# A Perceiver block: pools of their own for gates and ups, the last two pairs of chunks by sequence, and an early table of roots

## The chip, the cores and the metric

The kernel runs on one core of a Trainium2 chip. The metric is device time in microseconds (us) of one execution, a median over runs. Beside the runs there is one profiled execution, whose trace gives start, length and waits of every instruction. The engines are TensorE (PE in the trace, PEld for its weight loads), VectorE (DVE), ScalarE (ACT), GpSimd (POOL) and SyncE (SP, which issues most of the transfers).

## The reference

Four sequences of 128 tokens with 1024 features pass through cross-attention over 8192 context rows, causal self-attention, and a feed-forward part, each behind a layernorm and added to its input. The change touches only the last part:

```python
gate_up = jnp.einsum('bsh,oh->bso', x, w_gu)
gate, up = (gate_up[..., :I], gate_up[..., I:])        # I = 2816
h = jax.nn.silu(gate) * up
y = jnp.einsum('bsi,hi->bsh', h, w_down)
rms = jnp.sqrt(jnp.mean(y * y, axis=-1, keepdims=True) + EPS)
return y / rms
```

The weights `w_gu` and `w_down` come packed in 4 bits with a scale for each group of 128. The block's output is x plus this.

## The kernel before

The kernel is one function, `tile_perceiver`. Its earlier stages (keys and values of the context, cross-attention, projections, self-attention) are issued in an order written out by hand: steps with a due time go to an agenda, which `perform()` issues sorted. The weights of the feed-forward part are unpacked meanwhile and kept in DRAM as f32 (`gu_d`, `dn_d`). The last step of the agenda is `first_gate_up` (L1253), the 48 matmuls of gate and up of the first chunk of inner features, into PSUM tiles of the pool `acc_ps`. After that the order within each engine is not written by hand: the framework orders the instructions from their dependencies, their place in the program and its own estimate of times, and it puts in all waits.

The 2816 inner features are 22 chunks of 128 (NI = 22). All 512 tokens (four sequences t of 128) are the moving operand of the gates and ups, so a gate or an up of one chunk is a tile of 128 features by 512 tokens.

Products are made of three matmuls, to get more precision than one gives: each f32 operand is split in a high part (ScalarE, L155), a low part (VectorE, L158) and a third part (VectorE, L159). The high and low products go to accumulator a, the third to accumulator b, and `join_into` puts them together: ScalarE scales a into `fa` (L1386), VectorE adds b (L1387).

The feed-forward part:

- `load_ffn` (L1378 and after) brings 128x1024 weights from DRAM (`fw_raw`, issued by SP) and splits them in `fw_h`, `fw_l` and `fw_d`. All these have two buffers.
- Chunk 0 is joined from `acc_ps` by `inner(0, ...)`. Then the pools `sa_ps` (transposes and values of self-attention: three tiles `pt` and one `po`, on the default side of PSUM) and `acc_ps` (two `a` and two `b`, on the right side) are closed, and `gu_ps` is opened, which takes all eight banks: gate_a, gate_b, up_a, up_b, two of each.
- For j = 1 to 21: load gate weights, 24 matmuls; load up weights, 24 matmuls (`matmul_halves`, L165); then `inner(j, ...)`: join gate, join up, sigmoid (L1411), two products (L1412, L1413) into `hT[j]`. For j under 8 (EARLY) `hT[j]` is split at once by `split_inner` (ScalarE L1399, VectorE L1400 to L1403).
- Then `gu_ps` is closed, the memory of `x3` and of the gates is given back, and the pools `ff_h` (SBUF) and `y_ps` (PSUM, eight banks: y_a and y_b for each of four sequences) are opened.
- The downs: for each half n of the 1024 output columns, for each of 11 pairs q of chunks: load the pair's weights, and for each sequence t six matmuls (L1454, two chunks by three parts). In the first half the remaining `hT` (8 to 21) are split along the way.
- After each half, for each t: join into `y` (L1387), Square with a sum over the columns (L1465). In the second half also: sum of both halves (L1468), mean (L1469), root on ScalarE (L1472), reciprocal (L1473), and for both halves the final step `y * ms + x1` (L1476) and the transfer to the output (L1479).

ScalarE's root needs another table of functions than the sigmoid; a table load stands in the trace as ACT_TABLE_LOAD.

Of the kernel before, what the change touches and what calls it, by code (L numbers as in the profile page):

```python
# [34 lines left out]
F32 = mybir.dt.float32  # L35
# [5 lines left out]
AF = mybir.ActivationFunctionType  # L41
ALU = mybir.AluOpType
AX = mybir.AxisListType
PSUM = bass.MemoryType.PSUM
DRAM = bass.MemoryType.DRAM

P = 128
# [24 lines left out]
NI = INNER // P  # L72
# [14 lines left out]
def tile_perceiver(  # L87
# [26 lines left out]
    nc = tc.nc  # L114
# [15 lines left out]
    dn_d = dram.tile([2, NI // 2, P, 2, 512], F32, name="dn_d")  # L130
# [13 lines left out]
    def split(src, hi, lo, df):  # L144

        split_hi(src, hi)
        split_lo(src, hi, lo, df)
# [8 lines left out]
    def matmul_halves(a, b, lhs, rhs):  # L161

        for k in range(NC):
            for i, ps in enumerate((a, a, b)):
                nc.tensor.matmul(  # L165
                    ps,
                    lhsT=lhs(i, k),
                    rhs=rhs(i, k),
                    start=(k == 0 and i != 1),
                    stop=(k == NC - 1 and i != 0),  # L170
                )
# [41 lines left out]
    w3 = {0: [], 1: []}  # L213
# [489 lines left out]
    first, last = V_QUANT  # L703
# [30 lines left out]
    with tc.tile_pool(name="at_e", bufs=1) as at_e, tc.tile_pool(  # L734
        name="at_s", bufs=4
    ) as small, tc.tile_pool(name="at", bufs=2) as at, tc.tile_pool(
        name="at_ps", bufs=3, space=PSUM
# [219 lines left out]
        with tc.manual_schedule():  # L957
            for s in range(n_steps + LAG_V):
                n, g = divmod(s, NSC)
# [9 lines left out]
                if n < len(units):  # L969
                    h, t = units[n]  # L970
# [43 lines left out]
    w3s = {}  # L1014
# [356 lines left out]
    with tc.tile_pool(name="ff_t", bufs=2) as ff_t, tc.tile_pool(name="ff", bufs=1) as ff:  # L1371
        hT = [ff.tile([P, 512], F32, name=f"hT{j}", tag=f"hT{j}") for j in range(NI)]
        ss = ff.tile([P, NT, 2], F32, name="ss")

        def load_ffn(src, n):

            raw = ff_t.tile([P, C], F32, name="fw_raw", tag="fw_raw")
            nc.sync.dma_start(out=raw.rearrange("p (i n) -> p i n", n=n), in_=src)  # L1378
            parts = [ff_t.tile([P, C], F32R, name=f"fw_{c}", tag=f"fw_{c}") for c in "hld"]
            split(raw, *parts)  # L1380
            return [t.rearrange("p (i n) -> p i n", n=n) for t in parts]

        def join_into(dst, a, b):

            fa = ff_t.tile([P, 512], F32, name="fa", tag="fa")
            nc.scalar.mul(fa, a, 1.0 + 1.0 / UP)  # L1386
            nc.vector.scalar_tensor_tensor(dst, b, -1.0 / UP, fa, ALU.mult, ALU.add)  # L1387

        def joined(pool, a, b, name):
            t = pool.tile([P, 512], F32, name=name, tag=name)  # L1390
            join_into(t, a, b)
            return t


        h3 = {}

        def split_inner(pool, j):
            hi, lo = (pool.tile([P, 512], F32R, name=f"h3_{c}{j}") for c in "hl")
            nc.scalar.mul(hi, hT[j], 1.0 - 0.5 / UP)  # L1399
            nc.vector.tensor_tensor(lo, hT[j], hi, ALU.subtract)  # L1400
            nc.vector.tensor_scalar_mul(lo, lo, UP)
            df = ff.tile([P, 512], F32R, name=f"h3_d{j}", tag=f"hT{j}")
            nc.vector.tensor_tensor(df, hi, lo, ALU.subtract)  # L1403
            h3[j] = [hi, lo, df]

        with tc.tile_pool(name="ff_g", bufs=2) as ff_g:

            def inner(j, gate_ab, up_ab):
                gate, up = joined(ff_g, *gate_ab, "gate"), joined(ff_g, *up_ab, "up")
                sg = ff_g.tile([P, 512], F32, name="sg", tag="sg")  # L1410
                nc.scalar.activation(sg, gate, AF.Sigmoid)  # L1411
                nc.vector.tensor_tensor(sg, sg, gate, ALU.mult)  # L1412
                nc.vector.tensor_tensor(hT[j], sg, up, ALU.mult)  # L1413
                if j < EARLY:
                    split_inner(ff, j)

            inner(0, acc["ff", 0], acc["ff", 1])
            sa_ps_s.close()
            acc_s.close()
            with tc.tile_pool(name="gu_ps", bufs=2, space=PSUM) as gu_ps:  # L1420
                for j in range(1, NI):
                    gu = []
                    for i, name in enumerate(("gate", "up")):
                        w3 = load_ffn(gu_d[2 * j + i], P)
                        ab = [
                            gu_ps.tile([P, 512], F32, name=f"{name}_{c}", tag=f"{name}_{c}")
                            for c in "ab"
                        ]
                        matmul_halves(
                            *ab, lambda i, k: w3[i][:, k, :], lambda i, k: x3[i][:, :, k, :]  # L1430
                        )
                        gu.append(ab)
                    inner(j, *gu)
        x3_s.close()

        with tc.tile_pool(name="ff_h", bufs=1) as ff_h, tc.tile_pool(
            name="y_ps", bufs=1, space=PSUM
        ) as y_ps:
            y = ff_h.tile([P, NT, C], F32, name="y")
            for n in range(2):  # L1440
                yab = [
                    [y_ps.tile([P, 512], F32, name=f"y{t}_{c}", tag=f"y{t}_{c}") for c in "ab"]
                    for t in range(NT)
                ]
                for q in range(NI // 2):
                    w3 = load_ffn(dn_d[n, q], 512)
                    if n == 0:
                        for j in range(2 * q + 2, min(2 * q + 4, NI)):
                            if j >= EARLY:
                                split_inner(ff_h, j)  # L1450
                    for t in range(NT):
                        for j in (2 * q, 2 * q + 1):
                            for i, ps in enumerate((yab[t][0], yab[t][0], yab[t][1])):
                                nc.tensor.matmul(  # L1454
                                    ps,
                                    lhsT=h3[j][i][:, ts(t, P)],
                                    rhs=w3[i][:, j % 2, :],
                                    start=(j == 0 and i != 1),
                                    stop=(j == NI - 1 and i != 0),
                                )  # L1460
                for t in range(NT):
                    yt = y[:, t, ts(n, 512)]
                    join_into(yt, *yab[t])
                    sqr = ff_h.tile([P, 512], F32, name="sqr", tag="sqr")
                    nc.scalar.activation(sqr, yt, AF.Square, accum_out=ss[:, t, n : n + 1])  # L1465
                    if n == 1:
                        ms = ff.tile([P, 1], F32, name="ms", tag="ms", bufs=NT)
                        nc.vector.tensor_tensor(ms, ss[:, t, 0:1], ss[:, t, 1:2], ALU.add)  # L1468
                        nc.vector.tensor_scalar(  # L1469
                            ms, ms, 1.0 / C, 1e-6 / FP4_UP**2, ALU.mult, ALU.add  # L1470
                        )
                        nc.scalar.activation(ms, ms, AF.Sqrt)  # L1472
                        nc.vector.reciprocal(ms, ms)  # L1473
                        for m in range(2):
                            yt = y[:, t, ts(m, 512)]
                            nc.vector.scalar_tensor_tensor(  # L1476
                                yt, yt, ms, x1[:, t, ts(m, 512)], ALU.mult, ALU.add
                            )
                            nc.sync.dma_start(out=out[ts(t, P), ts(m, 512)], in_=yt)  # L1479
# [71 lines left out]
```

## Time and profile before

| what | us |
|---|---|
| median of 3 runs (2878.3 to 2881.0) | 2880.05 |
| profiled execution, its own time | 2883.89 |
| its span, first to last instruction | 2882.1 |
| TensorE busy in the span | 2666.1 (93%) |
| VectorE busy | 2418.6 (84%) |
| ScalarE busy | 1266.1 (44%) |
| first gate matmul of chunk 1 starts | 2508.8 |
| last up matmul starts | 2743.9 |
| last down matmul starts | 2870.5 |

Times in the trace count from the first instruction. In a row of the trace's groups stand line, engine, operation, output and inputs, shape and count, then busy time and mean length of one, and after the second bar how long the engine had been idle just before those instructions and what ended that. Matmuls overlap their neighbours, so a length of 394 ns is longer than the distance of two starts; distances of starts are the better measure of TensorE's pace.

### The profile page before, as it was taken

How to read it: one execution, taken by the hardware profiler on the slowest of the kernel's cores; microseconds unless marked ns; L12 is line 12 of the kernel's file. 1: busy time of each engine (PE TensorE's matmuls, PEld its weight loads, DVE VectorE, ACT ScalarE, POOL GpSimd, SP SyncE). 2: the span in 40 equal slices, each digit the busy share in tenths (PEclk: the TensorE clock that was granted, in tenths of full speed). 3: DMA queues.
4: the chain of work that ended last, by engine and by line, in shares of the span. 5: the costliest groups of instructions: out<-in, count | busy, mean ns of one | idle time of the engine just before them, and what ended most of it. 6: DMA issues, size and time to landing. Idle time of an engine off the chain costs nothing.

```text
span 2882.1 us, 41034 instructions
## 1 busy us (share of the span) xinstructions
PE 2666.1 (93%) x15480; PEld 2067.8 (72%) x15480; DVE 2418.6 (84%) x3959; ACT 1266.1 (44%) x1399; POOL 454.6 (16%) x608
## 2 busy tenths in 40 slices
PE   8999999999999999999987877787778899799998
PEld 3788888888888888888864555555555777688876
DVE  6899999555799989898879999999986898676674
ACT  4211212121323333333219999999983245333332
POOL 0011111000012222222122233322311000000000
PEclk9999999999999999999998999999999999899999
DMA  5555565222348777777437788878882322122222
GB/s 186 168 198 199 199 211 211 95 95 95 135 125 205 193 191 186 192 181 198 108 87 162 143 167 163 170 161 154 159 167 87 95 70 67 52 95 92 92 91 91
DMA packets 452711, 413.17 MB, mean 143 GB/s; under 512 B 356953, under 2 KB 361625, under 8 KB 452513
## 3 DMA queue, kind: packets, MB, share of 16 engines
q1 hardware_dynamic: 404928, 252.22, 36.6%
q0 software_dynamic: 46528, 157.29, 17.2%
q8 instruction: 121, 1.98, 0.3%
q10 hardware_dynamic: 1056, 1.05, 0.2%
q14 instruction: 78, 0.63, 0.1%
HBM read 220.14 MB, written 104.34 MB: 113 GB/s over the span
## 4 chain that ended last, share of the span: by engine, by line
PE 71%; DVE 20%; issue 4%; POOL 2%; ACT 1%; DMA 1%; SPq 0%; DVEq 0%; ACTq 0%; POOLq 0%
PE kv_a L342 33%; PE kv_b L342 16%; DVE e L787 13%; PE acc_a L1100 3%; PE y_a L1454 3%; PE gate_a L165 3%; PE up_a L165 3%; POOL sk L760 2%; PE acc_b L1100 2%; PE y_b L1454 1%; PE gate_b L165 1%; PE up_b L165 1%; PE q_ps L292 1%; PE a_pt L830 1%; PE sc L780 1%
## 5 line engine op out<-in xcount | busy, mean ns | idle before, releaser
L342 PE MATMUL kv_a<-w_h,c_h 128*128 128x512 f32 x2048 | 806.3, 394 | 0.0
L342 PE MATMUL kv_a<-w_l,c_l 128*128 128x512 f32 x2048 | 806.0, 394 | 0.2 <-ACT w_l L246 0.2
L342 PE MATMUL kv_b<-w_d,c_d 128*128 128x512 f32 x2048 | 806.0, 394 | 0.0
L787 DVE CUSTOM_DVE_ANT_0 e<-sc,sk 128x1024 f32<-128x1024 f32 x512 | 593.2, 1219 | 8.8 <-PE sc L780 7.7
L815 ACT ACTIVATE a<-e,m,sqs 128x4096 int16<-128x4096 f32 x128 | 486.9, 3804 | 25.2 <-DVE m L804 24.8
L342 PEld LDWEIGHTS kv_a<-w_l,c_l 128*128 128x128 f32 x2048 | 384.8, 188 | 89.6 <-ACT w_l L246 0.6
L342 PEld LDWEIGHTS kv_a<-w_h,c_h 128*128 128x128 f32 x2048 | 384.9, 188 | 88.9 <-issue 0.2
L342 PEld LDWEIGHTS kv_b<-w_d,c_d 128*128 128x128 f32 x2048 | 384.8, 188 | 88.9 <-DVE c_d L159 0.3
L155 ACT ACTIVATE c_h<-c_raw 128x1024 fp32r<-128x1024 f32 x128 | 135.1, 1057 | 415.8 <-PE kv_a L342 413.5
L356 DVE SCALAR_TENSOR_TENSOR f<-kv_a,bkv 128x512 f32<-128x512 f32 x256 | 175.6, 686 | 163.3 <-PE kv_a L342 162.6
L780 PE MATMUL sc<-kt,qT 64*128 64x512 bf16 x1024 | 207.4, 397 | 102.5 <-DVE mx L787 98.5
L581 ACT CAST kst<-kT 128x512 bf16<-128x512 int16 x128 | 89.4, 698 | 309.0 <-DMA kT<-ki 309.0
L830 PE MATMUL a_pt<-ident,a 128*128 128x128 f32 x1024 | 176.5, 297 | 20.7 <-ACT a L815 16.1
L357 DVE SCALAR_TENSOR_TENSOR f<-kv_b,f 128x512 f32<-128x512 f32 x256 | 176.6, 690 | 20.3 <-DVE f L356 0.9
L760 POOL PARTITION_BROADCAST sk<-sk_row x120 | 142.5, 1297 | 312.9 <-DVE mx L787 312.7
L830 PEld LDWEIGHTS a_pt<-ident,a 128*128 128x128 f32 x1024 | 113.0, 146 | 87.2 <-ACT a L815 48.6
L780 PEld LDWEIGHTS <-qT 64*128 64x128 bf16 x1024 | 74.8, 93 | 130.9 <-issue 101.2
L158 DVE TENSOR_TENSOR fw_l<-fw_raw,fw_h 128x1024 fp32r<-128x1024 f32 x64 | 78.2, 1223 | 107.1 <-ACT fw_h L155 106.9
L158 DVE TENSOR_TENSOR c_l<-c_raw,c_h 128x1024 fp32r<-128x1024 f32 x128 | 155.6, 1215 | 6.2 <-ACT c_h L155 5.9
L159 DVE SCALAR_TENSOR_TENSOR c_d<-c_l,c_raw 128x1024 fp32r<-128x1024 f32 x128 | 156.2, 1220 | 2.3
L155 ACT ACTIVATE fw_h<-fw_raw 128x1024 fp32r<-128x1024 f32 x64 | 67.8, 1061 | 179.7 <-PE y_a L1454 75.1
L548 ACT CAST vq<-vi 128x1024 f16<-128x1024 int16 x64 | 66.9, 1046 | 174.2 <-DVE vi L541 128.8
(203 smaller groups left out, 4114.1 us busy)
## 6 DMA issues: line engine op xcount, KB each, us to landing
c_raw<-in_ctxT SPq DMA_DIRECT2D x128, 512.0 KB, 3.6
v_d<-f POOLq DMA_DIRECT2D x64, 512.0 KB, 3.1
vl<-v_d POOLq DMA_DIRECT2D x64, 512.0 KB, 4.2
gu_d<-w_ffn POOLq DMA_DIRECT2D x44, 512.0 KB, 3.1
fw_raw<-gu_d SPq DMA_DIRECT2D x42, 512.0 KB, 3.4
k_d<-kst POOLq DMA_DIRECT2D x128, 128.0 KB, 3.5
vq_d<-vq POOLq DMA_DIRECT2D x32, 512.0 KB, 5.3
kt<-k_d SPq DMA_DIRECT2D x64, 256.0 KB, 3.6
```

Source lines behind the costliest of these rows:

```text
L155: nc.scalar.mul(hi, src, 1.0 - 0.5 / UP)
L158: nc.vector.tensor_tensor(lo, src, hi, ALU.subtract)
L159: nc.vector.scalar_tensor_tensor(df, lo, -1.0 - UP, src, ALU.mult, ALU.add)
L165: nc.tensor.matmul(ps, lhsT=lhs(i, k), rhs=rhs(i, k), start=(k == 0 and i != 1), stop=(k == NC - 1 and i != 0),)
L342: nc.tensor.matmul(ps, lhsT=tokens[s][i][:, k, :], rhs=w3[s < KT][k][i][:, ts(n, 512)], start=(k == 0 and i != 1), stop=(k == NC - 1 and i ...
L356: nc.vector.scalar_tensor_tensor(f, a, 1.0 + 1.0 / UP, bias[s < KT][n], ALU.mult, ALU.add)
L357: nc.vector.scalar_tensor_tensor(f, b, -1.0 / UP, f, ALU.mult, ALU.add)
L760: nc.gpsimd.partition_broadcast(tile_of_scales(h, g), sks_at[h][32 * c : 32 * c + 1, ts(half, SC)], channels=P)
L780: nc.tensor.matmul(ps[:, ts(i, 512)], lhsT=qT[rows, h, ts(t, P)], rhs=kts[h, g // 2][rows, ts(g % 2, 512)], start=True, stop=True,)
L787: nc.vector.tensor_tensor_reduce(out=state[n]["e"][-1][:, ts(g % (NSC // NEC), SC)], in0=ps, in1=sks_at[h, g], scale=1.0, scalar=LOWEST, o ...
L815: nc.scalar.activation(a, st["e"][c], AF.Exp, bias=st["m"], scale=sqs[:, 0, t, h : h + 1], accum_out=sums[h][:, t, c : c + 1],)
L830: nc.tensor.transpose(pt[:, i, :], a[:, at_word + P * i : at_word + P * i + P], ident)
```

## The change

It has four parts.

1. `gu_ps` becomes two pools, `g_ps` for the gates and `u_ps` for the ups, each with two buffers for each tag (four banks), opened in this order.
2. `y_ps` becomes two pools: `y_ps` for sequences 0 and 1 and `y2_ps` for 2 and 3, four banks each, opened in this order.
3. The downs are cut in two functions, `load_down(q)` and `down(q, t)`. In the first half of the columns all is called in the same order as before. In the second half, pairs 0 to 8 are as before; then the weights of pairs 9 and 10 are both loaded, and the eight calls for these two pairs come in the order (9,0), (9,1), (9,2), (10,0), (9,3), (10,1), (10,2), (10,3), as (pair, sequence).
4. After the first Square of the first half, one root of a single column is taken, whose result nothing reads.

```diff
-            with tc.tile_pool(name="gu_ps", bufs=2, space=PSUM) as gu_ps:
+            with tc.tile_pool(name="g_ps", bufs=2, space=PSUM) as g_ps, tc.tile_pool(
+                name="u_ps", bufs=2, space=PSUM
+            ) as u_ps:
                 for j in range(1, NI):
                     gu = []
-                    for i, name in enumerate(("gate", "up")):
+                    for i, (name, gu_ps) in enumerate((("gate", g_ps), ("up", u_ps))):
...
         with tc.tile_pool(name="ff_h", bufs=1) as ff_h, tc.tile_pool(
             name="y_ps", bufs=1, space=PSUM
-        ) as y_ps:
+        ) as y_ps, tc.tile_pool(name="y2_ps", bufs=1, space=PSUM) as y2_ps:
             y = ff_h.tile([P, NT, C], F32, name="y")
             for n in range(2):
                 yab = [
-                    [y_ps.tile([P, 512], F32, name=f"y{t}_{c}", tag=f"y{t}_{c}") for c in "ab"]
+                    [
+                        (y_ps, y2_ps)[t // 2].tile([P, 512], F32, name=f"y{t}_{c}", tag=f"y{t}_{c}")
+                        for c in "ab"
+                    ]
                     for t in range(NT)
                 ]
-                for q in range(NI // 2):
-                    w3 = load_ffn(dn_d[n, q], 512)
+                w3s = {}
+
+                def load_down(q):
+                    w3s[q] = load_ffn(dn_d[n, q], 512)
                     if n == 0:
                         for j in range(2 * q + 2, min(2 * q + 4, NI)):
                             if j >= EARLY:
                                 split_inner(ff_h, j)
+
+                def down(q, t):
+                    for j in (2 * q, 2 * q + 1):
+                        for i, ps in enumerate((yab[t][0], yab[t][0], yab[t][1])):
+                            nc.tensor.matmul(
+                                ps,
+                                lhsT=h3[j][i][:, ts(t, P)],
+                                rhs=w3s[q][i][:, j % 2, :],
+                                start=(j == 0 and i != 1),
+                                stop=(j == NI - 1 and i != 0),
+                            )
...
+                last = NI // 2 - 1
+                together = last if n == 0 else last - 2
+                for q in range(together + 1):
+                    load_down(q)
                     for t in range(NT):
...
+                        down(q, t)
+                for q in range(together + 1, last + 1):
+                    load_down(q)
+                if n == 1:
+                    for q, t in ((0, 0), (0, 1), (0, 2), (1, 0), (0, 3), (1, 1), (1, 2), (1, 3)):
+                        down(last - 1 + q, t)
                 for t in range(NT):
                     yt = y[:, t, ts(n, 512)]
                     join_into(yt, *yab[t])
                     sqr = ff_h.tile([P, 512], F32, name="sqr", tag="sqr")
                     nc.scalar.activation(sqr, yt, AF.Square, accum_out=ss[:, t, n : n + 1])
+                    if n == 0 and t == 0:
+
+                        nc.scalar.activation(sqr[:, 0:1], ss[:, 0, 0:1], AF.Sqrt)
```

More of the change, by code (lines that the diff above doesn't have):

```diff
@@ L1450, in tile_perceiver @@
                                 split_inner(ff_h, j)
-                    for t in range(NT):
[L1452 to L1460, printed above, removed]
+                def down(q, t):
[12 more added lines that the diff above has]
+                    load_down(q)
+                    for t in range(NT):
+                        down(q, t)
[4 more added lines that the diff above has]
+                        down(last - 1 + q, t)
                 for t in range(NT):
```

## The prediction

> **What bounds the kernel now.** I read the page's busy shares first, then the groups of instructions for the stretch that the change touches (2440 us to the end), then busy time by window, then the timelines of TensorE, VectorE and ScalarE at the places where TensorE is idle. The busy shares say TensorE 93% (2666.1 of 2882.1 us), VectorE 84%, ScalarE 44%. The change touches only the feed-forward part, about the last 380 us, so the question is where TensorE stands still in it. The groups, kept apart by shape:
>
> ```profile
> L165 PE MATMUL gate_a<-x_h,fw_h 128*128 128x512 f32 x168 | 67.1, 400 | 1.5 <-DVE up L1387 1.5
> L165 PE MATMUL up_a<-x_h,fw_h 128*128 128x512 f32 x168 | 67.0, 399 | 0.0
> ...
> L1454 PE MATMUL y_a<-fw_h,h_h 128*128 128x512 f32 x176 | 70.0, 398 | 2.7 <-DVE up L1387 2.7
> ```
>
> Columns: busy us, mean ns of one, idle us just before, and what ended it. In 1008 gate and up matmuls and 528 down matmuls TensorE waits twice in all: 1.5 us before a gate and 2.7 us before a y, both ended by the VectorE join of an up (L1387). Everywhere else these stages run at TensorE's own pace: in a steady stretch matmuls start every 0.2333 us (gate, up) or 0.2311 us (down), since neighbours overlap. The windows agree:
>
> ```profile
> 2743.00:2752.00 9.00, 6.32 (x21) 4.75 (x20) 6.17 (x10) 4.82 (x9) 0.00 (x0) 0.81 0.37 118
> 2752.00:2805.00 53.00, 53.00 (x231) 43.02 (x230) 40.40 (x56) 14.73 (x18) 0.00 (x0) 1.00 0.27 90
> 2805.00:2815.00 10.00, 10.00 (x44) 8.09 (x44) 7.19 (x8) 5.80 (x14) 0.00 (x0) 1.00 0.21 66
> 2815.00:2866.00 51.00, 51.00 (x222) 41.39 (x221) 22.05 (x18) 9.52 (x9) 0.00 (x0) 1.00 0.23 80
> 2866.00:2882.10 16.10, 4.93 (x22) 3.67 (x20) 9.47 (x24) 6.65 (x17) 0.00 (x0) 0.73 0.34 130
> ```
>
> After the length come busy time of PE, PEld, DVE, ACT and POOL, then the granted clock. From 2752 to 2866 PE is busy all the time, also where the first half of the output columns gives way to the second (2805 to 2815). Time is lost where ups give way to downs (2743 to 2752, clock 0.81) and in the tail after 2866. The timeline of PE at the first of these:
>
> ```profile
> 2743.90 0.40 PE L165 MATMUL up_b<-x_d,fw_d 128*128 128x512 f32 x1
> 2746.97 0.61 PE L1454 MATMUL y_a<-fw_h,h_h 128*128 128x512 f32 x1 [2.68 <-DVE up L1387]
> 2747.38 0.63 PE L1454 MATMUL y_a<-fw_l,h_l 128*128 128x512 f32 x1
> 2747.81 0.63 PE L1454 MATMUL y_b<-fw_d,h_d 128*128 128x512 f32 x1
> ```
>
> To be seen: 3.07 us between two starts, then starts 0.43 us apart in place of 0.23. The tail, on ScalarE and then on VectorE:
>
> ```profile
> 2868.57 0.58 ACT L1386 ACTIVATE fa<-y_a 128x512 f32<-128x512 f32 x1
> 2869.16 1.28 ACT L1472 ACT_TABLE_LOAD   x1
> 2870.46 0.20 ACT L1472 ACTIVATE ms<-ms 128x1 f32<-128x1 f32 x1
> ```
> ```profile
> 2870.89 1.42 DVE L1476 SCALAR_TENSOR_TENSOR y<-y,ms,x 128x512 f32<-128x512 f32 x2
> ...
> 2877.53 1.41 DVE L1476 SCALAR_TENSOR_TENSOR y<-y,ms,x 128x512 f32<-128x512 f32 x2
> ```
>
> The table of roots is loaded between the last matmuls and the first final step of VectorE. From that step (2870.89) to the end of the last one (2878.94) VectorE is busy nearly without a break: the tail is VectorE's.
>
> **What the Trainium skill says.** "TensorE: Matmul & The Clock Gate", section "What's actually happening": an idle window of about 3.4 us lets the clock fall to half, and about 3.4 us of work bring it back. The trace agrees in kind: after a gap of 2.7 us, shorter than that window, eight spacings are 0.427 us, the figure that the page gives for 512 columns at half clock (section "Wait — 56ns, not 53.3ns?"). The page also says that the window runs freely, so a run without the profile may lose less. "ScalarE: Activation LUTs", section "What ACT_TABLE_LOAD costs": about 1283 ns; the trace has 1.28 us. Its section "Table sets: the hidden batching unit" says that a switch of set costs a load each time; here Square at 2870.57 runs after Sqrt without a second load, so the set with the root serves the rest.
>
> **The change, part by part.**
> A. *Start of the gates.* Before, gu_ps takes all eight banks, so its first gate waits for the last join of chunk 0. sa_ps (three pt and one po: four banks) lies on the default side, acc_ps (two a, two b) on the right. g_ps, opened first, should take sa_ps's four banks, last read at 2496.94 (x_d from pt). The first gate then follows the last matmul of first_gate_up (start 2506.98) at about 2507.22 in place of 2508.83: **-1.6 us**. Its weights have been split since 2483.16. The ups wait for acc_ps, read out by 2508.77, and start at 2507.22 + 24 x 0.2333 = 2512.8, so that wait is covered by 4 us. If banks lie otherwise: 0.
>
> B. *Ups to downs.* y_ps (sequences 0 and 1) should take g_ps's banks, whose last join ended by 2741.23; y2_ps takes the ups' and waits for the join at 2746.15 + 0.68 = 2746.83. The first down can start at 2743.90 + 0.23 = 2744.13; its weights (fw_d) are ready at 2742.36. Two sequences are 12 matmuls, 2.77 us; the third wants to start at 2746.90 and can at 2746.97: a wait of 0.07 us remains. Before, the tenth down matmul starts at 2750.70; after, at 2744.13 + 9 x 0.231 = 2746.21, less 0.07 for the wait: **-4.4 us** (2.8 from the idle, 1.6 from the slow clock). What is late next: weight splits and the splits of h on VectorE. The latter can't start before 2748.7 (their memory becomes free with the last hT), and VectorE is then full: about 5.35 us per pair of chunks beside TensorE's 5.55. The third pair's weights (ScalarE's fw_h after the first pair ends, then fw_l and fw_d) are ready at 2757.69 and needed at 2759.5 + 0.5 before. With TensorE 4.4 us early and VectorE's order as it is, only 1.24 + 0.43 us of VectorE's idle time can be squeezed out; the third and fifth pairs would be late by 1.3 to 1.6 us. If the order follows readiness (first pair ends at 2749.7, fw_h until 2750.8, at most one 1.3 us block ahead, 1.14 + 0.6 + 1.22 for fw_l, an h operation and fw_d), they are ready at about 2755.1 and needed at 2755.8, so nothing is late. I take 0 and keep 1.6 for the range, as the order on VectorE comes out of when things are ready: weight splits stand early among the h splits already in the trace. Gate and up keep two buffers for each tag, so their steady stage is unchanged.
>
> C. *The early root.* One table load and one 128x1 activation, 1.28 + 0.20 = 1.48 us, in the passage from columns 0 to columns 1, right after the first Square (ends 2808.08). ScalarE's later work there shifts: the third fa from 2808.32 to 2809.6, the weights of the next pair (2809.43) to about 2810.7, the fourth fa from 2811.00 to about 2812.2. The fourth join then ends near 2813.5, and its banks are wanted at 2809.4 + 18 x 0.231 = 2813.6; fw_d comes at about 2814.7 against 2815.0 + 0.4. So TensorE covers it narrowly: **+0.1 us**, bounds 0 and 1.5 (all of it on the path).
>
> D. *The last two pairs by sequence.* Pairs 9 and 10 are 8 calls of 6 matmuls, 1.39 us each. Before, sequence 0 ends three calls before the end; now four: 1.39 us earlier. Sequences 1 to 3 end as before. Both pairs must be split before call 4. Pair 10 reuses pair 8's buffers, and took 3.65 us from the end of pair 8 (2859.41 to 2863.06); three calls of pair 9 give 4.16 us, so it is hidden with 0.5 us to spare; SP's transfers of raw weights keep their order and releases. Without the table load, the chain of sequence 0 is fa (0.60), join (0.69), Square and its read (0.73), sum and mean (0.35), root (0.20), reciprocal (0.16) with about 0.03 between. Its fa starts at 2866.58 - 1.39 = 2865.19, so the first final step starts near 2868.1 in place of 2870.89, 2.8 us earlier. But VectorE had already joined sequence 1 before that step; now this (0.65 us) falls behind it. VectorE's stretch of 8.05 us becomes 8.7 and ends at 2876.8 in place of 2878.94: **-2.0 us** with rounding. Bounds: -1.4 (only the shift of sequence 0, the order of VectorE awkward) and -3.4 (then the last sequence's own chain from its last matmul binds). The output transfers follow the final steps as before.
>
> Sum: -1.6 - 4.4 + 0.1 - 2.0 = **-7.9 us**. The profiled execution took 2883.89 us (span 2882.1 and 1.8 around it); it would take 2876.0. The median of the runs shown is 2880.05, 3.8 us less, and I take the sum off this: **2872.2 us**, 0.27% less. Differences within 0.2% (5.8 us) count as no change, so the limit is 2874.3.
>
> **Rivals.**
> 1. *The feed takes the place of the PSUM wait.* TensorE gets its banks early and stands before weight splits: VectorE's order stays, 1.6 us go; or the unprofiled runs didn't lose all of the slow clock. 2880.05 - 7.9 + 1.8 = **2874.0**. For: VectorE has 0.2 us to spare per pair. Against: its weight splits come ahead of most h operations.
> 2. *The pools don't part the waits.* Were banks laid out so that y_ps still waits for the last up, A and B would be nothing: -2.0 + 0.1, **2878.1**. For: nothing in the trace names banks. Against: the first gate waited for acc_ps although its first bank should be sa_ps's, free 12 us before, so waits go with the whole pool.
> 3. *Slower: the h splits move ahead of the third pair's weights on VectorE.* Place: pair 2 of the first half. Each h tile is 1.54 us of VectorE (0.60 + 0.34 + 0.60), from 2749.4 on. With all 14 ahead, the weights are ready at 2749.4 + 21.6 + 2.4 = 2773.4, 17.6 us after TensorE wants them (2755.8), and the clock falls again (1.65): 19.2 - 7.9 = +11.3, **2891**. It beats the gain from seven tiles on and passes the limit of 0.2% at twelve. For: ScalarE does seven h_h in one block (2748.72) ahead of fw_h of the third pair. Against: VectorE had only two h tiles ahead, and an earlier end of the first pair makes the weights ready sooner.
>
> **How the numbers follow.** Forecast 0.64 with its own range of 2870 to 2874.5; rival 1 0.15; rival 2 0.12; rival 3 0.09. Faster by over 0.2%: nearly all of the forecast and half of rival 1, 0.70; slower by over 0.2%: nearly all of rival 3, 0.08; the rest, 0.22, within. Low end: B 4.4, A 1.6, D 3.4 and C 0 give -9.4, and 1.5 us for the spread of the runs (2878.3 to 2881.0): 2869. High end 2877.5: it takes in rival 1 and the lower bounds of B, C and D together (-1.6 - 2.8 + 1.5 - 1.4 = -4.3, or 2875.7) and leaves out rivals 2 and 3.
>
> **What would show it.** A: the gate group's idle falls from 1.5 to about 0. B: the y group's idle from 2.7 to under 0.2, spacing 0.23 us from the first down on, clock near 1.00 around the passage; a new idle on y naming fw_l or fw_d would be rival 1 or 3, one still naming up before the first y rival 2. C: a table load at the passage to columns 1 with no idle of PE after it. D: no table load in the tail, the first final step about 2.4 us before the last matmul starts (it was 0.35 us after); from the last matmul's start (2870.54 before) to the end of the last final step 6.3 us in place of 8.4. Wrong would be a tail that is shorter by less than 1.4 us, or TensorE idle in the down stage for over 1 us.

## The result, and the profile after

| | before | after |
|---|---|---|
| median (13 runs each) | 2880.05 | 2871.46 |
| lowest to highest | 2871.25 to 2884.82 | 2868.0 to 2873.35 |
| profiled execution, own time | 2883.89 | 2872.01 |
| its span | 2882.1 | 2870.2 |

The ratio of the times, after over before, is 0.9971 with a 95% interval of 0.9963 to 0.9978: faster by 0.29% (0.22 to 0.37), or 6.3 to 10.7 us. The forecast was 2872.2 us, 7.9 us less.

The groups of the kernel after, for 2440 us to the end, kept apart by shape:

```profile
L165 PE MATMUL gate_a<-x_h,fw_h 128*128 128x512 f32 x168 | 65.9, 392 | 0.0
L165 PE MATMUL up_a<-x_h,fw_h 128*128 128x512 f32 x168 | 65.9, 392 | 0.0
...
L1463 PE MATMUL y_a<-fw_h,h_h 128*128 128x512 f32 x176 | 69.5, 395 | 0.0
```

Both idle times, 1.5 us before a gate and 2.7 us before a down (now L1463), are gone, and no other group of gates, ups or downs in this stretch has any. The windows over the same stages as in the prediction (moved with the earlier start):

```profile
2737.00:2746.00 9.00, 9.00 (x40) 7.09 (x40) 6.30 (x9) 4.95 (x8) 0.00 (x0) 1.00 0.36 118
2746.00:2799.00 53.00, 53.00 (x230) 42.84 (x229) 43.57 (x61) 17.40 (x24) 0.00 (x0) 1.00 0.27 91
2799.00:2809.00 10.00, 10.00 (x45) 8.09 (x44) 6.29 (x6) 5.10 (x12) 0.00 (x0) 1.00 0.27 99
2809.00:2856.00 47.00, 47.00 (x204) 38.00 (x203) 19.88 (x17) 9.08 (x9) 0.00 (x0) 1.00 0.23 79
```

The passage from ups to downs (first row) went from 6.32 of 9 us busy at a clock of 0.81 to 9 of 9 at 1.00. The timeline of TensorE there:

```profile
2737.77 0.39 PE L165 MATMUL up_b<-x_d,fw_d 128*128 128x512 f32 x1
2738.00 0.40 PE L1463 MATMUL y_a<-fw_h,h_h 128*128 128x512 f32 x1
2738.23 0.40 PE L1463 MATMUL y_a<-fw_l,h_l 128*128 128x512 f32 x1
...
2740.56 0.40 PE L1463 MATMUL y_b<-fw_d,h_d 128*128 128x512 f32 x1
2740.80 0.46 PE L1463 MATMUL y_a<-fw_h,h_h 128*128 128x512 f32 x1
2741.10 0.40 PE L1463 MATMUL y_a<-fw_l,h_l 128*128 128x512 f32 x1
```

Downs follow ups 0.23 us later. The thirteenth down (2740.80) is by the program's order the first of the third sequence, and so the first on the second of the two new pools, `y2_ps`: its step to the next start is 0.30 us in place of 0.23. These 0.07 us are probably what is left of the wait for the join of the last up, which ends at 2740.70. The table load has moved to the passage from columns 0 to columns 1, and there is none in the tail any more:

```profile
2797.80 1.28 ACT L1490 ACT_TABLE_LOAD   x1
```

The tail, on VectorE:

```profile
2858.03 1.42 DVE L1501 SCALAR_TENSOR_TENSOR y<-y,ms,x 128x512 f32<-128x512 f32 x2
2859.36 1.30 DVE L1387 SCALAR_TENSOR_TENSOR y<-y_b,fa 128x512 f32<-128x512 f32 x2
2860.84 0.16 DVE L1493 TENSOR_TENSOR ms<-ss 128x1 f32<-128x1 f32 x1 [0.18 <-ACT sqr L1487]
...
2861.36 0.69 DVE L1387 SCALAR_TENSOR_TENSOR y<-y_b,fa 128x512 f32<-128x512 f32 x1 [0.17 <-ACT fa L1386]
...
2865.63 1.42 DVE L1501 SCALAR_TENSOR_TENSOR y<-y,ms,x 128x512 f32<-128x512 f32 x2
```

The last down matmul starts at 2860.47. The first final step comes 2.44 us before that (0.35 us after it in the kernel before), and the last ends 6.58 us after it (8.40 before).

Where the two profiles part, stage by stage, from starts in the two timelines:

| stage | before | after | difference |
|---|---|---|---|
| start to the first matmul of `first_gate_up` | 2494.22 | 2490.09 | -4.13 |
| from there to the first gate | 14.61 | 12.71 | -1.90 |
| to the last up | 235.07 | 234.97 | -0.10 |
| to the tenth down | 6.80 | 2.33 | -4.47 |
| to the last down | 119.84 | 120.37 | +0.53 |
| to the end of the last final step | 8.40 | 6.58 | -1.82 |
| to the end of the span | 3.16 | 3.15 | -0.01 |

The first row isn't the change's: up to there every engine runs the same instructions in the same order. In the fourteen profiles (these two and all twelve experiments, alike up to there) that point lies between 2487.52 and 2496.59 us. So two spans differ by up to 9.1 us for nothing that the change does, and the parts of the change are better read from distances inside the feed-forward part. The +0.53 of the downs is mostly not the change's either: in e10, e11 and e12 below, whose downs are the same as here, they take 119.92 to 119.96 us, 0.1 more than before; in the profile of the kernel after all downs start a little further apart (0.2322 us in the mean from the 101st to the last, against 0.2313 in these three).

### The profile page after: what moved, and what is told of

Its sections match the earlier page's. It is cut to its first block, busy times and chain, and to the rows that moved or that the text cites. A ratio compares the mean times of both kernels' runs of the same rounds, so it can differ in the third digit from the quotient of the medians.

```text
span 2870.2 us, 41035 instructions
## 1 busy us (share of the span) xinstructions
PE 2661.8 (93%) x15480; PEld 2065.8 (72%) x15480; DVE 2421.4 (84%) x3959; ACT 1266.0 (44%) x1400; POOL 455.9 (16%) x608
## 4 chain that ended last, share of the span: by engine, by line
PE 72%; DVE 19%; issue 4%; POOL 2%; DMA 1%; ACT 1%; DVEq 0%; ACTq 0%; SPq 0%; POOLq 0%
PE kv_a L342 33%; PE kv_b L342 16%; DVE e L787 13%; PE acc_a L1100 3%; PE gate_a L165 3%; PE up_a L165 3%; PE y_a L1463 3%; PE q_ps L292 2%; POOL sk L760 2%; PE acc_b L1100 2%; PE up_b L165 1%; PE gate_b L165 1%; PE y_b L1463 1%; PE a_pt L830 1%; PE sc L780 1%
```

## The experiments

All start from the kernel after unless said otherwise. "Tail" is the time from the start of the last down matmul to the end of the last final step, "passage" that from the last up to the tenth down. Each was timed beside the kernel before on the same chip. The median of the kernel before was 2879.12 us beside e1 to e4, 2880.99 beside e5 to e8 and 2880.73 beside e10 to e13, so the ratios are to be compared and not the medians.

**The down pools put together again (e2_one_y).**

```diff
-        ) as y_ps, tc.tile_pool(name="y2_ps", bufs=1, space=PSUM) as y2_ps:
+        ) as y_ps:
...
-                        (y_ps, y2_ps)[t // 2].tile([P, 512], F32, name=f"y{t}_{c}", tag=f"y{t}_{c}")
+                        y_ps.tile([P, 512], F32, name=f"y{t}_{c}", tag=f"y{t}_{c}")
```

> Gates and ups keep their own pools, but the downs go back to one pool of eight banks. If waits go with the whole pool: no idle before the first gate, 2.7 us before the first down and the slow spacing after it, 4.4 us longer than the changed kernel, near 2875.9. Rival: a tile waits only for what lay on its own bank: the first down (on a gate's bank) starts at once, any wait comes at the third sequence and is under 0.2 us, 2871.5.

Measured: 2874.31, ratio 0.9978 (0.9971 to 0.9985). There is no idle before the first gate, but 2.68 us before the first down:

```profile
2738.83 0.47 PE L1463 MATMUL y_a<-fw_h,h_h 128*128 128x512 f32 x1 [2.68 <-DVE up L1387]
2739.14 0.40 PE L1463 MATMUL y_a<-fw_l,h_l 128*128 128x512 f32 x1
2739.38 0.39 PE L1463 MATMUL y_b<-fw_d,h_d 128*128 128x512 f32 x1
```

Here the gates and the ups had four banks each. On VectorE the last join of a gate ends at 2733.09, that of an up at 2738.69, so half of the banks had been read out long before, and the weights were there. TensorE stands still for 2.68 us and no down starts until the ups' join, though the framework takes what is ready first (e1, below, shows that). So a new pool waits as a whole, for all that lay in its memory, and not tile by tile. (The traces don't name the bank of a tile.) But the slow spacing isn't there: the starts are 0.31 and 0.24 us apart. The passage is 5.25 us, not 6.80. The expectation had taken the slow clock for a fixed price of the idle; see the last section.

**The down pools alone parted (e13_y_split_only).** From the kernel before: part 2 without part 1, 3 and 4.

> The kernel before with the down pool alone parted (part 2), gates and ups in one pool. If waits go with a whole pool, both down pools lie on the one pool of gates and ups and wait for its last join: 1.5 us idle before the first gate and 2.7 us before the first down as before, 2880. Rival: the second pool is what counts, idle before the first down under 0.3 us, 2876. The spacing after the idle (0.43 or 0.23 us) is a further sample of whether an idle of 2.7 us always ends in the slow clock.

Measured: 2880.32, ratio 0.9999 (0.9991 to 1.0006). Idle 1.5 us before a gate and 2.7 us before a down. Both new pools waited for the last join of an up, so the old pool is given back as a whole too. (This takes it that one of the two new pools lay on the gates' banks, which the traces don't show.) Without the split of the pool that comes before, the split of the pool that comes after is worth nothing here. The slow clock came late, after two starts:

```profile
2741.49 0.47 PE L1461 MATMUL y_a<-fw_h,h_h 128*128 128x512 f32 x1 [2.68 <-DVE up L1387]
2741.80 0.44 PE L1461 MATMUL y_a<-fw_l,h_l 128*128 128x512 f32 x1
2742.03 0.63 PE L1461 MATMUL y_b<-fw_d,h_d 128*128 128x512 f32 x1
2742.46 0.63 PE L1461 MATMUL y_a<-fw_h,h_h 128*128 128x512 f32 x1
```

**Ups' pool opened first (e1_u_first).**

```diff
-            with tc.tile_pool(name="g_ps", bufs=2, space=PSUM) as g_ps, tc.tile_pool(
-                name="u_ps", bufs=2, space=PSUM
-            ) as u_ps:
+            with tc.tile_pool(name="u_ps", bufs=2, space=PSUM) as u_ps, tc.tile_pool(
+                name="g_ps", bufs=2, space=PSUM
+            ) as g_ps:
```

> The two pools of ups and gates opened in the other order (ups first), nothing else. If a pool waits for everything that lay on its banks, and banks are given from the default side upwards, the gates now lie on the banks of the accumulators of chunk 0 and the first down pool on the ups' banks: TensorE idles about 1.5 us before the first gate and about 2.7 us before the first down, and the first downs run at the slow spacing of 0.43 us; 6 us longer than the changed kernel, near 2877.5. Rival: it is the parting alone that counts, not which banks: no idle, 2871.5.

Measured: 2870.56, ratio 0.9968 (0.9955 to 0.9981), no idle before a gate, an up or a down. The theory's number was missed, by 7 us, and the rival's was met. What the theory had left out is that the order on TensorE isn't written by hand here, and the framework fills the wait:

```profile
2502.19 0.39 PE L165 MATMUL up_b<-x_d,fw_d 128*128 128x512 f32 x1
2502.43 0.40 PE L165 MATMUL up_a<-x_h,fw_h 128*128 128x512 f32 x1
2502.66 0.48 PE L165 MATMUL gate_a<-x_h,fw_h 128*128 128x512 f32 x1
```

Seven ups of chunk 1 go ahead of its gates, the other 17 come after them. The first gate starts at 2502.66, 0.08 us after the join of the up of chunk 0, so the gates did wait as the theory had it, and the ups did not. The first downs don't wait either. That they are those of sequences 2 and 3, on the gates' banks, would explain it, but the trace doesn't name the sequence of a down, so this isn't shown. Two pools leave something that is ready; which of them is free first didn't matter.

**The pools alone (e5_pools_only).** Parts 1 and 2 in the kernel before, without the order and the root.

> The kernel before with the pools alone parted (parts 1 and 2). Theory: no idle of TensorE before the first gate and the first down, spacing 0.23 us throughout, tail of 8.4 us as before: 6.0 us less than before, 2874. Rival: weight splits are late in the first half of the downs, idle of 1 to 2 us there, 2876.

Measured: 2873.96, ratio 0.9975 (0.9966 to 0.9983), no idle, passage 2.33 us, tail 8.41. The rival's late weight splits don't appear.

**The h splits ahead of the third pair's weights (e8_h_first).** This brings about the prediction's slower rival:

```diff
-                        for j in range(2 * q + 2, min(2 * q + 4, NI)):
-                            if j >= EARLY:
+                        for j in range(EARLY, NI):
+                            if q == 1:
                                 split_inner(ff_h, j)
```

> The changed kernel with all 14 splits of h of the first half issued before the weights of the third pair. This is the slower rival of the prediction made on purpose: if VectorE then takes them first, the third pair's weights come 15 to 18 us late, TensorE idles that long in the third pair and starts again at the slow spacing: near 2890. Rival: what is ready goes first, so weight splits still slip in between: under 3 us idle, 2874 or less.

Measured: 2892.13, ratio 1.0033 (1.0013 to 1.0052). In the groups of its downs:

```profile
L1463 PE MATMUL y_a<-fw_l,h_l 128*128 128x512 f32 x176 | 69.8, 398 | 13.9 <-DVE fw_l L158 13.9
L1463 PE MATMUL y_a<-fw_h,h_h 128*128 128x512 f32 x176 | 69.5, 398 | 1.6 <-ACT fw_h L155 1.6
```

TensorE waits 15.5 us for fw_h and fw_l of the third pair, and VectorE's timeline has the 14 h tiles in one block from 2749.57 to 2771.13 ahead of them. From the tenth down to the last it takes 137.57 us, 17.6 more than in e10 to e12 below; the prediction had 19.2 for this. The feed of the downs can become the bound; in the kernel after it doesn't:

```profile
2743.26 1.29 DVE L1400 TENSOR_TENSOR h_l<-hT,h_h 128x512 fp32r<-128x512 f32 x2 [0.82 <-ACT h_h L1399]
2744.47 0.42 DVE L1401 TENSOR_SCALAR h_l<-h_l 128x512 fp32r<-128x512 f32 x1
2744.81 1.22 DVE L158 TENSOR_TENSOR fw_l<-fw_raw,fw_h 128x1024 fp32r<-128x1024 f32 x1
```

There the third pair's fw_l starts after three h operations, 0.1 us after its input fw_h is ready (2744.71). All three parts of that pair's weights are there at 2747.77, and the last of them is wanted at 2749.71.

**Without the root, without the order, and each alone (e3_no_root, e4_no_order, e6_order_only, e7_root_only).** e3 leaves out the root of part 4. e4 sets `together` to `last` in both halves, so that the eight calls at the end go by pair. e6 and e7 are the kernel before with part 3 or part 4 alone.

> The changed kernel without the early root. Theory: the table load of 1.28 us comes back between the first Square of the tail and its root, overlaps 0.4 us of sum and mean, and the first final step starts 0.9 us later, the last ends 0.9 us later (0.6 to 1.3): 2872.4. TensorE has no new idle. Rival: the load is hidden in the tail too, since sequence 0 now is early: 0 us.

> The changed kernel with the last two pairs in the order of before. Theory: sequence 0 ends 1.39 us later, but VectorE joins sequence 1 ahead of the first final step again; from the last matmul's start to the end of the last final step 7.3 to 8.0 us in place of 6.6, 2872.5. Rival: VectorE's total work sets the end whatever the order, so the full 1.4 us come back: 8.0 us, 2872.9; or nothing, as the last sequence's own chain decides: 6.6 us.

> The kernel before with the order of the last two pairs alone (part 3). Theory: TensorE idles 1.5 and 2.7 us as before; tail 0.5 to 1.2 us shorter than 8.4; 2879. Rival: with the table load still in the tail the earlier end of sequence 0 is used up by it: 0 us, 2880.

> The kernel before with the early root alone (part 4). Theory: the tail is 0.7 to 1.4 us shorter than 8.4, TensorE isn't idle where columns 0 give way to columns 1; 2879. Rival: the 1.48 us on ScalarE at that place delay the fourth join and with it TensorE by up to 1.5 us: 2880.5.

| kernel | order | root | tail | median | ratio |
|---|---|---|---|---|---|
| before | no | no | 8.40 | 2880.05 | |
| e7_root_only | no | yes | 7.61 | 2882.03 | 0.9997 (0.9989 to 1.0006) |
| e6_order_only | yes | no | 7.47 | 2879.95 | 0.9998 (0.9989 to 1.0006) |
| after | yes | yes | 6.58 | 2871.46 | 0.9971 (0.9963 to 0.9978) |
| e3_no_root (pools parted) | yes | no | 7.46 | 2872.83 | 0.9973 (0.9957 to 0.9988) |
| e4_no_order (pools parted) | no | yes | 7.62 | 2872.93 | 0.9977 (0.9968 to 0.9986) |
| e5_pools_only | no | no | 8.41 | 2873.96 | 0.9975 (0.9966 to 0.9983) |

The tails repeat to 0.02 us in kernels with the same end, whatever the pools. The root alone takes 0.79 us off, the order alone 0.93, both 1.82, about the sum: they are two steps of one chain. For the tail all four expectations hold: 0.88 us longer without the root (0.9 expected), 7.62 us without the order (7.3 to 8.0), 0.93 shorter with the order alone (0.5 to 1.2) and 0.79 with the root alone (0.7 to 1.4). In whole times 0.8 or 0.9 us are 0.03%, and no interval here is narrower than 0.13%: the times of e6 and e7 neither show nor deny it. So of the gain in whole time only the part of the pools is shown (e5, with an interval that leaves out 1); the tail's part is shown in the traces alone. In e7 TensorE has no idle where columns 0 give way to columns 1, and its idle of 1.4 and 2.7 us at the other two places is as before.

**A shorter tail tried (e10_final_act, e12_final_act3, e11_final_pool2).** The final steps moved off VectorE in part; e10:

```diff
+                            if m == 0:
                                 nc.vector.scalar_tensor_tensor(
                                     yt, yt, ms, x1[:, t, ts(m, 512)], ALU.mult, ALU.add
                                 )
+                            else:
+                                nc.scalar.mul(yt, yt, ms)
+                                nc.gpsimd.tensor_tensor(yt, yt, x1[:, t, ts(m, 512)], ALU.add)
```

e12 has `m == 0 and t < 3` for ScalarE and GpSimd, and the rest on VectorE; e11 has GpSimd multiply and add for `m == 1 and t < 2`.

> The changed kernel, with the second half of each final step (y * ms + x1) taken off VectorE: ScalarE multiplies by ms, GpSimd adds x1. If VectorE's amount of work sets the tail, its part after the first final step falls by 4 x 0.7 us, and the last sequence's own chain decides, now longer by ScalarE's 0.6 and GpSimd's 1.25 us in place of 0.7: from the last matmul's start to the last final step 5.2 to 5.8 us in place of 6.6, total 1 us less, 2870.4. Rival: ScalarE and GpSimd start the extra steps late, tail 6.6 or more, 2871.5 to 2873.

> As the run with ScalarE and GpSimd, but it is the first half of the final step that moves, and only for sequences 0 to 2; the last sequence stays on VectorE. If VectorE's work sets the tail: 3 x 0.7 us less, tail 4.6 to 5.2 us, total 1.5 us less, 2870. Rival: ScalarE's extra 0.6 us each delay the Squares of later sequences and with them the last one: tail 5.5 to 6.6.

> The changed kernel, with the second half of the final step of sequences 0 and 1 on GpSimd alone, as a multiplication and an addition of about 1.25 us each. VectorE has 1.4 us less: tail 5.2 us in place of 6.6, 2870.1. Rival: GpSimd[...] ends last: tail 7 us or more.

Measured: e10 2874.93, ratio 0.9977 (0.9970 to 0.9984); e12 2875.3, 0.9982 (0.9974 to 0.9989); e11 2873.19, 0.9966 (0.9953 to 0.9979). None is shown to be better than the change (0.9963 to 0.9978). All three expectations failed. They had a tail of 5.2 to 5.8, 4.6 to 5.2 and 5.2 us; the last final step, on whichever engine, ends 7.01 us (e10), 6.60 (e12) and 7.44 (e11) after the start of the last down, against 6.58 in the kernel after. These are the rivals' tails, though not for e11's reason: VectorE ends last there, and GpSimd 3.4 us before it. Up to the end of the span it is 13.76, 12.16 and 10.85 us, against 9.76. The traces name two reasons. The first, in e10's groups for the tail:

```profile
L1502 DVE SCALAR_TENSOR_TENSOR y<-y,ms,x 128x512 f32<-128x512 f32 x4 | 3.9, 981 | 0.1
L1387 DVE SCALAR_TENSOR_TENSOR y<-y_b,fa 128x512 f32<-128x512 f32 x4 | 2.8, 688 | 3.3 <-ACT fa L1386 3.3
```

VectorE's final step takes 981 ns in the mean, 750 in the kernel after. The timelines of VectorE and of GpSimd show which ones are slow:

```profile
2864.42 0.75 DVE L1502 SCALAR_TENSOR_TENSOR y<-y,ms,x 128x512 f32<-128x512 f32 x1
...
2865.88 1.29 DVE L1502 SCALAR_TENSOR_TENSOR y<-y,ms,x 128x512 f32<-128x512 f32 x1
```
```profile
2865.36 1.26 POOL L1507 TENSOR_TENSOR y<-y,x 128x512 f32<-128x512 f32 x1 [2.21 <-ACT y L1506]
```

The step beside GpSimd's addition takes 1.29 us, the one before it 0.75. The slow steps end 0.55 us after the addition beside them (2867.17 after 2866.62, and 2869.02 after 2868.48), as if they had waited for it. ScalarE's multiplication isn't the cause: it runs beside the fast step too, from 2864.57. This agrees with the Trainium skill, "SBUF — State Buffer", section "Who interferes with whom": a VectorE instruction with two inputs from SBUF contends with a GpSimd instruction that reads SBUF. The joins (L1387, one input from PSUM) keep their 0.69 us, at 2862.59 beside GpSimd's first addition too. The second reason: the program ends late after GpSimd's work. From the end of GpSimd's last addition to the end of the span it takes 6.76 us in e10 (2870.14 to 2876.9), 6.79 in e12 (2869.51 to 2876.3) and 6.73 in e11 (2863.67 to 2870.4), while it takes 3.15 us after VectorE's last step in the kernel after. What fills it is GpSimd's closing DRAIN, an instruction that the framework puts at the end. In e10, with lengths in ns (least, median, most) and the first and last start:

```profile
L1576 POOLq DRAIN  x3: 52/93/7460, 2868.7 to 2876.6; - x3
```

The long one ends 5.97 us after the last addition in all three kernels, and only then do the engines meet for the end. In e10 and e12 this comes 3.6 and 2.2 us after SyncE is through with the output transfers, in e11 0.2 us.

## Why the prediction was right

- **A, the start of the gates: -1.6 predicted.** The idle of 1.5 us is gone. The stage went down by 1.90 us; the distance from the last matmul of `first_gate_up` to the first gate, 1.85 before, is now 0.23, which is the 1.6, and the rest is the pace at which `first_gate_up` began (its 16 high-part matmuls take 5.69 us before and 5.40 after), which the change doesn't touch: in the experiments they take from 5.20 us (e8) to 6.00 (e5).
- **B, ups to downs: -4.4 predicted, -4.47 measured.** The reason, that waits go with a whole pool, was an inference from one wait. e2 shows it for the pool that is opened and e13, with its proviso, for the one that is closed; with both sides parted no idle is left (e5). But 1.6 of the 4.4 us is the slow clock, and that isn't there in every execution: of five profiles with this idle of 2.68 us, the passage is 6.80, 6.65, 6.64, 6.61 and 5.25 us. So the part is worth 2.9 to 4.5 us.
- **The feed of the downs: 0 predicted, 0 measured.** The reason holds as put: the weight splits moved up with their readiness, and the third pair's weights are there 1.9 us before they are wanted (0.7 predicted). The bound of 1.6 us wasn't needed. The cost that rival 3 names is real where its order is forced, as e8 shows: predicted 2891 with all 14 tiles ahead, measured 2892.13. (By the rival's own figures the limit of 0.2% is passed at eleven tiles, not twelve.)
- **C, the early root: +0.1 predicted, 0 measured.** TensorE has no idle at the passage between columns. The cover is thin, but not where the prediction had it, which gave the fourth join 0.1 us. The framework put that join ahead of the next pair's weights: it ends at 2801.61, and its banks are wanted 18 starts after the first down of columns 1 (2799.40), near 2803.6. Now the weights have the least to spare: fw_d of the next pair is ready at 2804.97 and wanted at 2805.44. (The prediction read the start of columns 1 in the kernel before as 2809.4; it is 2809.68.)
- **D, the tail: -2.0 predicted, -1.82 measured.** (The prediction's own figures, 2878.94 to 2876.8, give -2.1.) The first final step came 2.44 us before the last matmul, 2.4 predicted. The term that was off is VectorE's stretch: 8.7 us predicted, 9.02 measured (2858.03 to 2867.05), since VectorE waits twice in it, 0.18 and 0.17 us, where the prediction had it busy throughout.
- **The sum: -7.9 predicted.** The parts give -1.6 - 4.5 - 1.8 = -7.9 us in the profiles (all rows of the table after the first: -7.8), and the medians differ by 8.6 with an interval of 6.3 to 10.7. That it is so near is partly luck: B has the slow clock in full, which one of five profiles didn't have, and the spread of 9.1 us ahead of the changed part, from profile to profile, is as large as the gain.

## What to carry to other kernels

Where two stages use the same memory and a pool waits, and is waited for, as a whole, make pools as fine as the order in which their users finish, on both sides of where they meet. The split of gates and ups alone (e2) did away with the first wait and not the second, and the split of the downs alone (e13) with neither. A short idle of TensorE costs its own length and perhaps the slow clock after it (here 1.4 to 1.6 us more after 2.68, in four of five profiles). In a tail, count the work of the engine that ends last from its first step on, look at what a helper engine does to its speed, and at what follows the helper's last instruction: GpSimd's closing DRAIN costs nothing as long as its last work lies well ahead of the end.

## What the runs showed of the hardware that was not expected

- An idle of the same 2.68 us was followed by slow matmuls (0.43 us apart) in four of five profiles, in numbers from six to eight, once only after two starts at 0.31 and 0.23 us (e13), and by none in e2. The idle of 1.45 us before the gates was followed by none in the four profiles that have it. That it varies fits the Trainium skill's free-running window ("TensorE: Matmul & The Clock Gate", "What's actually happening"). Its length doesn't: the page lets the clock fall after an idle window of about 3.4 us, and here 2.68 us of idle, 3.07 from start to start, were enough.
- GpSimd's closing DRAIN ends 5.97 us after its last tensor instruction in all fourteen profiles. In the eleven without GpSimd in the tail that instruction lies 536 to 554 us before the end (in the kernel before it ends at 2337.60), so that the DRAIN costs nothing there. Why it takes so long isn't shown.
- A single final step of VectorE took 0.75 us alone and up to 1.63 us beside GpSimd's multiplication and addition (e11, from 2860.92), more than twice as long.
